# A convolution, Gram and batch-norm kernel: filter weights loaded with z, two idle products, and the first channel's second convolution in two halves

## The chip, the cores and the metric

The kernel runs on one core of a Trainium2 chip. The core has TensorE (matrix products; PE in the profile, with its weight loads shown apart as PEld), VectorE (DVE), ScalarE (ACT), GpSimd (POOL) and SyncE (SP), and 16 DMA engines that move data between device memory and the on-chip memory. The metric is the device time of one execution in microseconds (us). The runs of the kernel before took 885.52, 881.20 and 883.17 us, so the median is 883.17 us.

## The reference, cut to what matters

The input x has 4 images, 64 channels and 256 x 256 pixels. Layer 0 convolves every channel with a filter that is a product of a vector over rows and a vector over columns. Both vectors come from a small network with sine activations that is applied to 256 positions:

```python
def filt(z, w1, b1, w2, b2, w3, b3, wo, freq, t, deltas):     # z: 256 x 33
    h = sin(freq * (z @ w1 + b1))
    h = sin(freq * (h @ w2 + b2))
    h = sin(freq * (h @ w3 + b3))
    return (h @ wo) * exp(-t * abs(deltas))                    # 256 x 64 channels
hx, hy = filt(z, X...), filt(z, Y...)
k = outer(hx[:, c], hy[:, c])                                  # per channel
y = causal_conv2d(x, k) / 512 + x * bias[c]                    # by FFT in the reference
# layer 1
scores = y @ y.T / sqrt(256)                                   # per image and channel
y2 = y + (scores * weights[c]).sum(-1, keepdims=True)
out = batch_norm(y2) * gamma[c] + beta[c]                      # mean and variance per channel
```

## The kernel before

Since the filter is an outer product, a convolution is two products with triangular Toeplitz matrices, one along each axis. They are built of 64 x 64 blocks; the product of a block of rows with a block that would be zero is left out. All numbers are 32-bit floats, and one product in the code is two weight loads and two matmuls in the profile.

**Start.** Loads go out on two queues: SP's (`nc.sync`) and ScalarE's (`nc.scalar`). SP issues z^T (L85), the biases (L89), two decay tables (L99, L101), the image data `xt` of channel 0 in four parts (L72), a unit matrix, per-channel constants, the weights `w` of channel 0 and the image data of channel 1. ScalarE issues the first layer's weights (L87) and then the weights of the other layers (L90). Both networks, X and Y, run side by side as one block-diagonal network of 128 rows, in two halves of 128 positions. In each of three layers TensorE makes a product `ph` (L131), DVE adds the bias, scales to turns and takes off whole turns in three steps (L134 to L139; the scale `turns` is made from the biases at L123), and ScalarE takes the sine (L141). Then TensorE makes the filter rows of channel 0, repeated on all partitions (L147, a = 1 for the first convolution and then a = 0 for the second), and DVE multiplies each by its decay (L150). Four transfers (L155), two on each queue, lay the shifted copies out as channel 0's Toeplitz matrix `toep` on 64 partitions, and DVE copies it to the other 64 (L163). The filters of all channels (L158, L161) are written to device memory (L170), from where the other channels' matrices are read. Three products whose results nobody reads (`idle`, L167) stand on TensorE between this and the first convolution.

**Per channel.** `conv_z` makes the first convolution (L210) in two halves m of the result, and `copy_z` has ScalarE copy each half from PSUM (the matmul results' memory) to `z`, one copy for each half u of the partitions (L219). `conv_x0` makes the second convolution from z (L233): for each half m of the result and each block i it sums over four blocks k of z; k = 0, 1 are the first half of z and k = 2, 3 the second. DVE then adds bias times x (L240). `gram` makes the Gram blocks (L270), DVE weighs and sums them (L290 to L304), GpSimd sums over partitions (L312), and two channels later mean and variance are formed, and ScalarE normalizes and stores (L366, L406).

**Order.** The schedule is written out by hand: each engine works its instructions in the order of the code. In the loop of channel c, ScalarE first copies channel c + 1's Toeplitz matrix to the upper partitions (`copy_h`, L192); then come `conv_x0(c)`, `conv_z(c + 1)` and `gram(c)` on TensorE. The four loads of a Toeplitz matrix (`load_h`, L187) go on SP's queue, each between other loads; those of channel 1 stand before the loop. The eight PSUM banks after the start belong to one pool, `ps`, that hands them out in turn.

Of the kernel before, what the change touches and what calls it, by code (L numbers as in the profile page):

```python
# [8 lines left out]
F32 = mybir.dt.float32  # L9
AF = mybir.ActivationFunctionType  # L10
ALU = mybir.AluOpType
# [4 lines left out]
B, C, S = 4, 64, 256  # L16
P = 128
EMB = 33
# [3 lines left out]
H = P // 2  # L22
# [15 lines left out]
def conv_scores_bn_kernel(  # L38
# [1 line left out]
    tc: tile.TileContext,  # L40
    xT: bass.AP,
    wl: bass.AP,
    zT: bass.AP,
    fw: bass.AP,
    fb: bass.AP,
    decay: bass.AP,
# [11 lines left out]
    nc = tc.nc  # L58

    const = ctx.enter_context(tc.tile_pool(name="const", bufs=1))  # L60
# [5 lines left out]
    xts, ws, hs = {}, {}, {}  # L66
# [14 lines left out]


    ctx.enter_context(tc.manual_schedule())
    zT_sb = const.tile([EMB, S], F32, name="zT_sb")
    nc.sync.dma_start(zT_sb, zT)  # L85
    fw_sb = const.tile([P, 4, P], F32, name="fw_sb")
    nc.scalar.dma_start(fw_sb[:EMB, 0, :], fw[:EMB, 0, :])  # L87
    fb_sb = const.tile([P, 4], F32, name="fb_sb")
    nc.sync.dma_start(fb_sb, fb)  # L89
    nc.scalar.dma_start(fw_sb[:, 1:, :], fw[:, 1:, :])  # L90
    eps = const.tile([P, 1], F32, name="eps")
    nc.vector.memset(eps, BN_EPS)
    ones = const.tile([P, H], F32, name="ones")
# [12 lines left out]
    chan_sb = const.tile([P, 3, C], F32, name="chan_sb")  # L106
# [15 lines left out]
    with tc.tile_pool(name="fps", bufs=4, space=PSUM) as fps:  # L122
        nc.vector.tensor_scalar(turns, fb_sb[:, 3:4], 1.0 / (2.0 * math.pi), None, ALU.mult)  # L123

        halves = [zT_sb[:, bass.ts(n, P)] for n in range(2)]
        for layer in range(3):
            for n in range(2):
                rhs = halves[n]
                K = rhs.shape[0]
                ph = fps.tile([P, P], F32, tag="ph", name=f"ph_{layer}_{n}")  # L130
                nc.tensor.matmul(ph, lhsT=fw_sb[:K, layer, :], rhs=rhs, start=True, stop=True)  # L131

                a = wk.tile([P, P], F32, tag="fa", name=f"fa_{layer}_{n}")
                nc.vector.tensor_scalar(  # L134
                    a, ph, fb_sb[:, layer : layer + 1], turns, ALU.add, ALU.mult
                )
                k = wk.tile([P, P], F32, tag="fk", name=f"fk_{layer}_{n}")
                nc.vector.tensor_scalar(k, a, ROUND, None, ALU.add)  # L138
                nc.vector.scalar_tensor_tensor(a, k, ROUND, a, ALU.subtract, ALU.subtract)  # L139
                h = wk.tile([P, P], F32, tag="fh", name=f"fh_{layer}_{n}", bufs=4)  # L140
                nc.scalar.activation(h, a, AF.Sin, scale=-PI2)  # L141
                halves[n] = h
        for a in (1, 0):
            ph = fps.tile([P, S], F32, tag="ph0", name=f"ph0_{a}", bufs=3)
            for n in range(2):
                weights = fw_sb[:, 3, a * C : a * C + 1].to_broadcast([P, P])
                nc.tensor.matmul(  # L147
                    ph[:, bass.ts(n, P)], lhsT=weights, rhs=halves[n], start=True, stop=True
                )
            nc.vector.tensor_tensor(g0_sb[:, a, :S], ph, decay0_sb[:, a], ALU.mult)  # L150
            for n in range(2):
                row = g0_sb[H * n : H * n + 1, a, 32 * n :]
                src = bass.AP(row.tensor, row.offset, [row.ap[0], [1, 32], [1, S]])
                queue = nc.scalar if n else nc.sync
                queue.dma_start(hs[0][bass.ts(n, 32), a, :S], src)  # L155
        ph = fps.tile([P, S], F32, tag="ph0", name="ph_out", bufs=3)
        for n in range(2):
            nc.tensor.matmul(  # L158
                ph[:, bass.ts(n, P)], lhsT=fw_sb[:, 3, :], rhs=halves[n], start=True, stop=True
            )  # L160
        nc.vector.tensor_tensor(g_sb[:, :S], ph, decay_sb, ALU.mult)  # L161
        for a in (1, 0):
            nc.vector.tensor_copy(hs[0][H:, a, :S], hs[0][:H, a, :S])  # L163

        for n in range(3):
            idle = fps.tile([P, 3, P], F32, tag="idle", name=f"idle_{n}", bufs=1)
            nc.tensor.matmul(idle, lhsT=fw_sb[:, 3, :], rhs=fw_sb[:, 1:, :], start=True, stop=True)  # L167
    for a in (1, 0):
        queue = nc.scalar if a else nc.sync
        queue.dma_start(  # L170
# [25 lines left out]
    ps = ctx.enter_context(tc.tile_pool(name="ps", bufs=8, space=PSUM))  # L196

    st8, zs = {}, {}
# [22 lines left out]
    def conv_x0(c, z, parts=range(2)):  # L221


        xt = [xts[c, v] for v in range(2)]
        toep, x0 = hs[c], st8[c][0]
        for m in parts:
            p2 = [ps.tile([P, 2, S], F32, tag="ps", name=f"p2_{c}_{m}_{v}") for v in range(2)]
            for i in range(2):
                for k in range(4):
                    for t in range(4):  # L230
                        v, u = t % 2, t // 2
                        rows = bass.ts(v, H)
                        nc.tensor.matmul(  # L233
                            p2[v][bass.ts(u, H), i, : S - H * k],
                            lhsT=z[rows, u, k, bass.ts(2 * m + i, H)],
                            rhs=toep[rows, 0, H * k : S], start=(k == 0), stop=(k == 3),
                        )
            for v in range(2):
                part = bass.ts(m, 2)
                nc.vector.scalar_tensor_tensor(  # L240
                    x0[:, v, part], xt[v][:, part], chan_sb[:, 0, c : c + 1],
                    p2[v][:, :, ::-1], ALU.mult, ALU.add,
                )

    def begin(c):
        x0 = wk.tile([P, 2, 4, S], F32, tag="x0", name=f"x0_{c}", bufs=5)
# [192 lines left out]
    def last_channels(c):  # L439
# [6 lines left out]
        copy_h(c)  # L446
        finish(*fins[e - 1], 0, 1)
        conv_x0(p, zs.pop(p))
        load_w(c)
        minus_mean(moms[f])  # L450
# [25 lines left out]
        tot = sum_squares(q, mom_q)  # L476
        z = zs.pop(c)
        conv_x0(c, z, [0])
        mom_p = sm.tile([P, 8], F32, tag="mom", name=f"mom_{p}")
        add_red_of(p, 0, red_by_pe(p, 0), mom_p)  # L480
        conv_x0(c, z, [1])
        finish(*fins[e], 1, 0)
        finish(*fins[e], 1, 1)
# [62 lines left out]
    for c in range(C - 2):  # L546
        p, q, f, e = c - 1, c - 2, c - 3, c - 4
# [115 lines left out]
```

## Time and profile before

| | |
|---|---|
| runs | 885.52, 881.20, 883.17 us; median 883.17 us |
| profiled execution | 879.23 us, of which the span from first to last instruction is 877.3 us |
| granted TensorE clock, mean | 0.992 |
| TensorE busy / weight loads / DVE / ACT / POOL | 98% / 95% / 86% / 71% / 48% of the span |
| first matmul of the filter network | 2.69 us after the span's start |
| first product of channel 0's convolution | 15.96 us |
| first product of channel 1's convolution after the wait | 25.73 us |

The profile shows one execution. Its busy shares say how much of the span an engine worked. Its chain follows back from the last instruction what released each step. A row of the timeline has the start, the duration, the engine (a q behind the name is the engine's instruction queue, which issues transfers), the line, the operation, the tiles written and read, and in brackets how long the engine had been idle and what ended that. A row of the waits says who waited for whom, for how long in total, how often, and the longest. Tiles are named without their numbers, so `g0_sb` appears as `g_sb` and `decay0_sb` as `decay_sb`.

### The profile page before, as it was taken

To read this page: it belongs to the slowest core of one execution; us is meant where nothing else is said; L and a number is where in the kernel's file an instruction comes from. 1 tells how busy PE (TensorE), PEld (TensorE's weight loads), DVE (VectorE), ACT (ScalarE), POOL (GpSimd) and SP (SyncE) were. 2 spreads that over 40 slices of the span, in tenths; PEclk is the share of its full clock that TensorE was granted. 3 is DMA by queue.
4 is the path that set the end of the run, shared out by engine and by line. 5 is a ranking of instruction groups with operands and counts; after the bars stand their busy time and mean duration, and the time that the engine had idled before them with its cause. 6 is when DMAs were issued, how large, how long until landed. Compare 5 with 4: busy or idle time off the path is not lost.

```text
span 877.3 us, 55962 instructions
## 1 busy us (share of the span) xinstructions
PE 857.4 (98%) x24678; PEld 836.7 (95%) x24678; DVE 754.9 (86%) x2642; ACT 620.6 (71%) x1212; POOL 425.1 (48%) x195
## 2 busy tenths in 40 slices
PE   7999999999999999999999999999999999999993
PEld 5999999999999999999999999999999999999992
DVE  3578988988988898898898898898898898898885
ACT  2256767867777777777777777776776777776784
POOL 0236446446546546545545545645645645645600
PEclk9999999999999999999999999999999999999996
DMA  6623556565565655555555556555555555556534
GB/s 187 214 84 133 199 197 207 198 208 196 200 205 196 205 203 199 199 202 204 195 200 203 200 202 206 198 202 201 197 205 197 198 200 205 204 192 213 177 138 169
DMA packets 89914, 169.69 MB, mean 193 GB/s; under 512 B 10566, under 2 KB 11784, under 8 KB 89672
## 3 DMA queue, kind: packets, MB, share of 16 engines
q1 hardware_dynamic: 89116, 165.51, 54.8%
q8 instruction: 194, 3.18, 1.5%
q10 hardware_dynamic: 556, 0.61, 0.2%
q14 instruction: 48, 0.39, 0.1%
HBM read 98.18 MB, written 67.76 MB: 189 GB/s over the span
## 4 chain that ended last, share of the span: by engine, by line
PE 97%; DVE 1%; DMA 1%; ACT 0%; issue 0%; ACTq 0%; DVEq 0%
PE p L210 32%; PE g L270 32%; PE p L233 32%; PE rp L341 1%; PE rp L346 0%; DMA toep<-g_sb 0%; PE ph L131 0%; DVE x L355 0%; ACT o L406 0%; DMA fw_sb<-in_fw 0%; DVE fa L134 0%; DVE fa L139 0%; ACT z L219 0%; ACT fh L141 0%; DVE fk L138 0%
## 5 line engine op out<-in xcount | busy, mean ns | idle before, releaser
L312 POOL PARTITION_ALL_REDUCE rd<-sp x61 | 373.5, 6122 | 183.5 <-DVE sp L304 183.5
L233 PE MATMUL p<-toep,z 64*64 64x256 f32 (+3 forms) x8192 | 301.8, 296 | 0.1
L210 PE MATMUL p<-toep,xt 64*64 64x256 f32 (+3 forms) x8192 | 301.7, 296 | 0.1
L270 PE MATMUL g<-x 64*64 64x192 f32 (+1 forms) x8192 | 300.4, 296 | 0.1
L233 PEld LDWEIGHTS p<-toep,z 64*64 64x64 f32 x8192 | 292.5, 133 | 7.2 <-ACT z L219 0.6
L210 PEld LDWEIGHTS p<-toep,xt 64*64 64x64 f32 x8192 | 289.4, 133 | 7.4 <-PE idle L167 0.7
L270 PEld LDWEIGHTS g<-x 64*64 64x64 f32 x8192 | 287.6, 133 | 0.7 <-issue 0.4
L290 DVE SCALAR_TENSOR_TENSOR junk<-g,w 128x192 f32<-128x192 f32 x512 | 161.2, 352 | 82.7 <-PE g L270 82.7
L406 ACT ACTIVATE o<-x,sh,g 128x512 f32<-128x512 f32 x253 | 204.2, 811 | 3.1
L240 DVE SCALAR_TENSOR_TENSOR x<-xt,chan_sb,p 128x512 f32<-128x512 f32 x256 | 174.0, 741 | 8.1 <-PE p L233 8.1
L219 ACT COPY z<-p 128x512 f32<-128x512 f32 x256 | 134.4, 575 | 24.7 <-PE p L210 24.7
L366 ACT ACTIVATE sq<-x,mom 128x1024 f32<-128x1024 f32 x128 | 146.3, 1143 | 5.3 <-DVE x L355 2.0
L326 DVE SCALAR_TENSOR_TENSOR x<-x,rd 128x1024 f32<-128x1024 f32 x122 | 144.2, 1220 | 0.1
L304 DVE SCALAR_TENSOR_TENSOR sp<-eye_sb,red,pr 128x128 f32<-128x128 f32 x488 | 138.0, 345 | 0.0
L330 POOL PARTITION_ALL_REDUCE mom<-mom x61 | 24.3, 399 | 230.5 <-DVE x L326 226.4
L319 ACT COPY rd<-rd 64x512 f32<-64x512 f32 x61 | 37.5, 615 | 135.9 <-POOL rd L312 135.9
L294 DVE SCALAR_TENSOR_TENSOR pr<-g,w 128x256 f32<-128x256 f32 x256 | 107.6, 420 | 0.0
L192 ACT COPY toep<-toep 64x512 f32<-64x512 f32 x63 | 38.9, 617 | 33.1 <-DMA toep<-g_dram 24.2
L361 ACT ACTIVATE mom<-mom 128x1 f32<-128x1 f32 x62 | 18.2, 293 | 35.3 <-POOL mom L330 35.0
L290 DVE DVE_READ_ACCUMULATOR junk<-g,w 128x1 f32 x512 | 42.7, 83 | 0.0
L372 POOL PARTITION_ALL_REDUCE tot<-mom x62 | 29.7, 480 | 9.4 <-ACT sq L366 9.4
L366 ACT ACTIVATION_READ_ACCUMULATOR sq<-x,mom 128x1 f32 x128 | 23.9, 187 | 0.0
(60 smaller groups left out, 210.2 us busy)
## 6 DMA issues: line engine op xcount, KB each, us to landing
xt<-in_xT SPq DMA_DIRECT2D x256, 256.0 KB
out<-o SPq DMA_DIRECT2D x256, 256.0 KB
w<-in_wl SPq DMA_DIRECT2D x64, 320.0 KB
toep<-g_dram SPq DMA_DIRECT2D x252, 36.0 KB
g_dram<-g_sb SPq DMA_DIRECT2D x1, 320.0 KB
g_dram<-g_sb ACTq DMA_DIRECT2D x1, 320.0 KB
decay_sb<-in_decay SPq DMA_DIRECT2D x1, 256.0 KB
fw_sb<-in_fw ACTq DMA_DIRECT2D x1, 192.0 KB
```

The costliest lines, as they stand in the source:

```text
L210: nc.tensor.matmul(p1[u][bass.ts(v, H), k, : S - H * i], lhsT=xts[c, v][rows, i, bass.ts(2 * m + k, H)], rhs=toep[rows, 1, H * i : S], sta ...
L219: nc.scalar.copy(zs[c][:, u, bass.ts(m, 2), :], p1[u][:, :, ::-1])
L233: nc.tensor.matmul(p2[v][bass.ts(u, H), i, : S - H * k], lhsT=z[rows, u, k, bass.ts(2 * m + i, H)], rhs=toep[rows, 0, H * k : S], start=(k ...
L240: nc.vector.scalar_tensor_tensor(x0[:, v, part], xt[v][:, part], chan_sb[:, 0, c : c + 1], p2[v][:, :, ::-1], ALU.mult, ALU.add,)
L270: nc.tensor.matmul(gs[u][bass.ts(h, H), o, :], lhsT=xb[rows, v, i, m, :], rhs=xb[rows, v, i, t, :], start=(i == 0), stop=(i == 3),)
L290: nc.vector.scalar_tensor_tensor(junk, g[:, part, :], 1.0 / math.sqrt(S), w[:, 3 * n : 3 * n + 3, :], ALU.mult, ALU.mult, accum_out=red0[: ...
L294: nc.vector.scalar_tensor_tensor(pr[:, b].rearrange("p (t s) -> p t s", s=H), g[:, COL, :], 1.0 / math.sqrt(S), w[:, 6:10, :], ALU.mult, A ...
L304: nc.vector.scalar_tensor_tensor(sp[:, b, part], eye_sb, red0[:, b, n : n + 1], pr[:, b, part], ALU.mult, ALU.add,)
L312: nc.gpsimd.partition_all_reduce(rd.rearrange("p b s -> p (b s)"), sp.rearrange("p b s -> p (b s)"), P, RED.add)
L326: nc.vector.scalar_tensor_tensor(x0[:, v], x0[:, v], 1.0, rd[:, 2 * v, None, :].to_broadcast([P, 4, S]), ALU.mult, ALU.add, accum_out=mom[ ...
L366: nc.scalar.activation(sq, st8[c][0][:, v], AF.Square, bias=mom[:, 5:6], accum_out=mom[:, 6 + v : 7 + v])
L406: nc.scalar.activation(o, y, AF.Identity, bias=sh, scale=g)
```

## The change

Three things are changed. First, the host packs the first layer's weights and z^T into one array `zw`, which one transfer on SP's queue brings; the biases go first on ScalarE's queue, followed by the other three weights as one array. Second, two idle products are made instead of three. Third, `conv_x0` of channel 0 is a function of its own: it opens the PSUM tiles of both halves m at once, makes all products with the first half of z (k = 0, 1), and then all with the second (k = 2, 3), with the bias added to each m as soon as it is complete. The other channels keep their order; their bias addition moves to `add_bias`.

```diff
 
 
     ctx.enter_context(tc.manual_schedule())
-    zT_sb = const.tile([EMB, S], F32, name="zT_sb")
-    nc.sync.dma_start(zT_sb, zT)
-    fw_sb = const.tile([P, 4, P], F32, name="fw_sb")
-    nc.scalar.dma_start(fw_sb[:EMB, 0, :], fw[:EMB, 0, :])
+    zw_sb = const.tile([P, P + S], F32, name="zw_sb")
+    nc.sync.dma_start(zw_sb[:EMB], zw[:EMB])
     fb_sb = const.tile([P, 4], F32, name="fb_sb")
-    nc.sync.dma_start(fb_sb, fb)
-    nc.scalar.dma_start(fw_sb[:, 1:, :], fw[:, 1:, :])
+    nc.scalar.dma_start(fb_sb, fb)
+    fw_sb = const.tile([P, 3, P], F32, name="fw_sb")
+    nc.scalar.dma_start(fw_sb, fw)
     eps = const.tile([P, 1], F32, name="eps")
     nc.vector.memset(eps, BN_EPS)
     ones = const.tile([P, H], F32, name="ones")
...
     with tc.tile_pool(name="fps", bufs=4, space=PSUM) as fps:
         nc.vector.tensor_scalar(turns, fb_sb[:, 3:4], 1.0 / (2.0 * math.pi), None, ALU.mult)
 
-        halves = [zT_sb[:, bass.ts(n, P)] for n in range(2)]
+        halves = [zw_sb[:EMB, bass.ts(1 + n, P)] for n in range(2)]
         for layer in range(3):
             for n in range(2):
                 rhs = halves[n]
-                K = rhs.shape[0]
+                weights = fw_sb[:, layer - 1, :] if layer else zw_sb[:EMB, :P]
                 ph = fps.tile([P, P], F32, tag="ph", name=f"ph_{layer}_{n}")
-                nc.tensor.matmul(ph, lhsT=fw_sb[:K, layer, :], rhs=rhs, start=True, stop=True)
+                nc.tensor.matmul(ph, lhsT=weights, rhs=rhs, start=True, stop=True)
 
                 a = wk.tile([P, P], F32, tag="fa", name=f"fa_{layer}_{n}")
                 nc.vector.tensor_scalar(
...
         for a in (1, 0):
             ph = fps.tile([P, S], F32, tag="ph0", name=f"ph0_{a}", bufs=3)
             for n in range(2):
-                weights = fw_sb[:, 3, a * C : a * C + 1].to_broadcast([P, P])
+                weights = fw_sb[:, 2, a * C : a * C + 1].to_broadcast([P, P])
                 nc.tensor.matmul(
                     ph[:, bass.ts(n, P)], lhsT=weights, rhs=halves[n], start=True, stop=True
                 )
...
         ph = fps.tile([P, S], F32, tag="ph0", name="ph_out", bufs=3)
         for n in range(2):
             nc.tensor.matmul(
-                ph[:, bass.ts(n, P)], lhsT=fw_sb[:, 3, :], rhs=halves[n], start=True, stop=True
+                ph[:, bass.ts(n, P)], lhsT=fw_sb[:, 2, :], rhs=halves[n], start=True, stop=True
             )
         nc.vector.tensor_tensor(g_sb[:, :S], ph, decay_sb, ALU.mult)
         for a in (1, 0):
             nc.vector.tensor_copy(hs[0][H:, a, :S], hs[0][:H, a, :S])
 
-        for n in range(3):
+        for n in range(2):
             idle = fps.tile([P, 3, P], F32, tag="idle", name=f"idle_{n}", bufs=1)
-            nc.tensor.matmul(idle, lhsT=fw_sb[:, 3, :], rhs=fw_sb[:, 1:, :], start=True, stop=True)
+            nc.tensor.matmul(idle, lhsT=fw_sb[:, 2, :], rhs=fw_sb, start=True, stop=True)
     for a in (1, 0):
         queue = nc.scalar if a else nc.sync
         queue.dma_start(
...
     def conv_x0(c, z, parts=range(2)):
 
-        xt = [xts[c, v] for v in range(2)]
-        toep, x0 = hs[c], st8[c][0]
+        toep = hs[c]
+        if not c:
+            first_x0(z)
+            return
         for m in parts:
             p2 = [ps.tile([P, 2, S], F32, tag="ps", name=f"p2_{c}_{m}_{v}") for v in range(2)]
             for i in range(2):
...
                             lhsT=z[rows, u, k, bass.ts(2 * m + i, H)],
                             rhs=toep[rows, 0, H * k : S], start=(k == 0), stop=(k == 3),
                         )
-            for v in range(2):
-                part = bass.ts(m, 2)
-                nc.vector.scalar_tensor_tensor(
-                    x0[:, v, part], xt[v][:, part], chan_sb[:, 0, c : c + 1],
-                    p2[v][:, :, ::-1], ALU.mult, ALU.add,
-                )
+            add_bias(c, m, p2)
+
+    def add_bias(c, m, p2):
+        for v in range(2):
+            part = bass.ts(m, 2)
+            nc.vector.scalar_tensor_tensor(
+                st8[c][0][:, v, part], xts[c, v][:, part], chan_sb[:, 0, c : c + 1],
+                p2[v][:, :, ::-1], ALU.mult, ALU.add,
+            )
+
+    def first_x0(z):
+
+        toep = hs[0]
+        p2 = [
+            [ps.tile([P, 2, S], F32, tag="ps", name=f"p2_0_{m}_{v}") for v in range(2)]
+            for m in range(2)
+        ]
+        for half in range(2):
+            for m in range(2):
+                for i in range(2):
+                    for k in range(2 * half, 2 * half + 2):
+                        for t in range(4):
+                            v, u = t % 2, t // 2
+                            rows = bass.ts(v, H)
+                            nc.tensor.matmul(
+                                p2[m][v][bass.ts(u, H), i, : S - H * k],
+                                lhsT=z[rows, u, k, bass.ts(2 * m + i, H)],
+                                rhs=toep[rows, 0, H * k : S],
+                                start=(i == 0 and k == 0), stop=(i == 1 and k == 3),
+                            )
+                if half:
+                    add_bias(0, m, p2[m])
 
     def begin(c):
         x0 = wk.tile([P, 2, 4, S], F32, tag="x0", name=f"x0_{c}", bufs=5)
...
     dec = np.exp(-(deltas[:, None] * t[None])).astype(np.float32)
     decay = np.concatenate([dec, dec / np.float32(FFT)], 0)
 
-    fw = np.zeros((P, 4, P), np.float32)
+    zw = np.zeros((P, P + S), np.float32)
+    zw[:EMB, P:] = a["L0_conv_z"][0, ::-1].T
+    fw = np.zeros((P, 3, P), np.float32)
     fb = np.zeros((P, 4), np.float32)
     for i, n in enumerate("XY"):
         lo, hi = i * C, (i + 1) * C
-        fw[:EMB, 0, lo:hi] = a[f"L0_conv_{n}w1"]
-        fw[lo:hi, 1, lo:hi] = a[f"L0_conv_{n}w2"]
-        fw[lo:hi, 2, lo:hi] = a[f"L0_conv_{n}w3"]
-        fw[lo:hi, 3, lo:hi] = a[f"L0_conv_{n}wo"]
+        zw[:EMB, lo:hi] = a[f"L0_conv_{n}w1"]
+        fw[lo:hi, 0, lo:hi] = a[f"L0_conv_{n}w2"]
+        fw[lo:hi, 1, lo:hi] = a[f"L0_conv_{n}w3"]
+        fw[lo:hi, 2, lo:hi] = a[f"L0_conv_{n}wo"]
         for j, b in enumerate(("b1", "b2", "b3")):
             fb[lo:hi, j] = a[f"L0_conv_{n}{b}"]
         fb[lo:hi, 3] = a[f"L0_conv_{n}freq"][0]
...
     arrays = {
         "xT": xo.transpose(2, 1, 0, 5, 4, 3).reshape(C, 2, P, 4, S),
         "wl": wl,
-        "zT": a["L0_conv_z"][0, ::-1].T,
+        "zw": zw,
         "fw": fw,
         "fb": fb,
         "decay": decay[:, ::-1],
```

More of the change, by code (lines that the diff above doesn't have):

```diff
@@ L42, in conv_scores_bn_kernel @@
     wl: bass.AP,
-    zT: bass.AP,
+    zw: bass.AP,
     fw: bass.AP,
```

## The prediction

> **What bounds the kernel now.** I read the page's busy shares and its chain first, then the waits of TensorE, then the first 26 us as a timeline, because every line of the change acts there.
>
> ```profile
> PE 857.4 (98%) x24678; PEld 836.7 (95%) x24678; DVE 754.9 (86%) x2642; ACT 620.6 (71%) x1212; POOL 425.1 (48%) x195
> ...
> PE 97%; DVE 1%; DMA 1%; ACT 0%; issue 0%; ACTq 0%; DVEq 0%
> ```
>
> TensorE is busy for 98% of the span and carries 97% of the chain. From 52 us on its pieces repeat every 13.08 us (52.42, 65.50, 78.58 in the chain). So the end moves by what TensorE loses or wins before it settles into that rhythm, and by nothing else. The waits that ended TensorE's idle times, over the whole run, with totals in us, times and the longest:
>
> ```profile
> PE ph L131 <- DMA fw_sb<-in_fw: 2.7, 1, 2.7
> ...
> PEld p L233 <- ACT z L219: 0.6, 2, 0.3
> ...
> PEld p L210 <- ACT toep L192: 0.3, 1, 0.3
> ```
>
> The first is the load of the filter network, the second the x0 product of channel 0 waiting for z, the third the z product of channel 1 waiting for its Toeplitz matrix. After 26 us no wait of TensorE on a transfer is listed; the 2.4 us on DVE at L341 belong to the last channels, which stay as they are. The head of the timeline (start, duration, and in brackets the idle time before and what ended it):
>
> ```profile
> 0.72 0.64 ACTq L87 DMA_DIRECT2D fw_sb<-in_fw  x1
> 0.72 0.43 SPq L85 DMA_DIRECT2D zT_sb<-in_zT  x1
> ...
> 1.22 0.37 SPq L89 DMA_DIRECT2D fb_sb<-in_fb  x1
> ...
> 2.69 1.22 PE L131 MATMUL ph<-zT_sb,fw_sb 33*128 33x128 f32 x4 [2.69 <-DMA fw_sb<-in_fw]
> ...
> 3.66 0.15 DVE L123 TENSOR_SCALAR turns<-fb_sb 128x1 f32<-128x1 f32 x1 [2.50 <-DMA fb_sb<-in_fb]
> 3.93 0.41 DVE L134 TENSOR_SCALAR fa<-ph,fb_sb,turns 128x128 f32<-128x128 f32 x1
> ```
>
> The chain names TensorE ahead of the first fa at 3.93, but a product is two of the four matmuls, and cut at 3.2 us the timeline has the first two done after 0.79 us, at 3.48. What really came last is the bias load: it landed just before 3.66, turns took 0.15, and fa followed. Next, the pieces of the chain before 26 us that lie around the first Toeplitz matrix:
>
> ```profile
> 12.04 3.56 DMA toep<-g_sb
> 15.60 0.02 issue
> 15.62 0.30 DVE toep L163
> 15.92 0.04 issue
> 15.96 4.67 PE p L210 x128
> 20.62 1.06 ACT z L219 x2
> ```
>
> The transfer takes 3.56 us from its issue; the idle products (13.04, 2.86 us, so until 15.90) end just as the DVE copy does (15.91). Then the timeline around the step to channel 1:
>
> ```profile
> 25.06 0.62 ACT L192 COPY toep<-toep 64x512 f32<-64x512 f32 x1 [3.38 <-DMA toep<-g_dram]
> ...
> 25.73 0.40 PEld L210 LDWEIGHTS p<-toep,xt 64*64 64x64 f32 x10 [0.31 <-ACT toep L192]
> ```
>
> TensorE could have gone on at 25.42 and was held to 25.73 by a Toeplitz matrix whose last load landed shortly before 25.06.
>
> **Part 1, the loads.** SP loses the issues of zT (0.43) and the biases (0.37) and gains one of zw (0.43); ScalarE's queue still issues two, now the biases and the three other weights. The first matmul waited for the load issued on ScalarE's queue with 0.64 us of issue; the one on SP cost 0.43, so I put zw's landing, with rows half as long again, 0.15 us before 2.65. Products done: 2.69 - 0.15 + 0.79 = 3.33. The biases are issued at 0.72 instead of 1.22; at the same 2.44 us to landing they arrive at 3.16, turns and its gap to fa (3.93 - 3.66 = 0.27) end at 3.43. So fa starts at 3.43: 0.5 us sooner. Both ends: 0, if the biases or zw land as late as before, or if the big weight load, now beside a decay load that SP issues 0.41 us sooner, holds the second layer (first use 5.32 before, 4.8 then; no wait on it shows today); 0.7 if the biases take the 1.93 us of the load that was first on that queue and zw gains the whole 0.21. A loss up to 0.2 stays possible where the single load on few rows is slow. I take 0.5, as two rows point to it. ScalarE's own first work at 4.96 (then 4.4) lies behind its table load and warm-up, which end at 3.28: no price.
>
> The Trainium skill, "DMA: Bandwidth & Descriptors", section "Issuing engines are not separate DMA queues", says that issuing on another engine saves only the issuing sequencer's time. By it the biases gain the 0.5 us of queueing and no more, where the row of the first load on that queue would give 1.0; fa is then bound by the products within 0.1 us of it.
>
> **Part 2, two idle products.** The layers, DVE and ScalarE steps from 3.93 to 12.04 are a strict chain and keep their lengths, so toep is issued at 11.53. SP is free by then: its last wait, for w, ended before 11.0. The DMA engines are 56% and 38% busy from 12 to 14 us, no full backlog, so the 3.56 us stay and the first z product starts at 15.46. Ends: 0 (landing kept at 15.60 by the channel 1 loads) and 0.5. Three idle products would end at 15.40; two end about 14.4, or 14.9 if the first one is slower. Removing 0.97 us of them wins nothing here, as the transfer covers it; it opens a pause of 0.6 to 1.0 us on TensorE. Whether that costs clock:
>
> ```profile
> L167 PEld LDWEIGHTS idle<-fw_sb x6: 186/189/333, 12.8 to 15.1; 128*128 128x128 f32 x6
> ...
> L158 PEld LDWEIGHTS ph_out<-fh,fw_sb x4: 333/333/333, 12.0 to 12.6; 128*128 128x128 f32 x4
> ```
>
> Weight loads take 333 ns up to 12.83 and 186 to 189 from 14.02: the clock rises between them, after some 3 us of closely packed matmuls. I price the shorter filler at 0, ends 0 and +4.7 (the whole first product, 4.67 us, at half speed); 0 is nearer, as the packed matmuls from 9.84 are all still there.
>
> The Trainium skill, "TensorE: Matmul & The Clock Gate", Part 1, speaks against this edit: the clock is released only after a busy window of about 3.4 us that runs free of the kernel. By its rule the pause alone is harmless, but a window that catches the pause could put the release off; an estimate from the page is up to 1.7 us lost (half of 3.4), where the trace gives 0.
>
> **Part 3, x0 of channel 0.** Today products for k = 2, 3 stand in the first quarter of x0, and TensorE waits 0.28 and 0.29 us for the two copies of the second half of z. In the new order all products of k = 0, 1 go first: (256 + 192)/640 of the columns, 0.70 of about 4.36 us, so 3.05 us of work, while the copies end 1.31 us after x0 begins (21.68 against 20.37). The 0.57 us go. The bias additions on DVE (two of 0.75 us per half, first at 23.40) come in one group near 23.6 and end about 26.6; the Gram products need them at 28.8 or later, and DVE is otherwise idle. The four banks of PSUM open together leave the other four to z of channel 1, freed by copies long done: 0.
>
> **Part 4, what is late next.** TensorE reaches z of channel 1 at 25.42 - 0.5 - 0.57 = 24.35. Its Toeplitz copy, the end of a chain that starts at the filter's last product, moves by 0.5: it ends at 25.18 and TensorE goes on at 25.23. Then 0.57 of Part 3 turns into a longer wait and the gain is 0.50. But the last of its four loads, issued by 21.83 (four issues of 2.68 us from 19.15), landed some 3 us later, and in 22.5 to 24.5 us this lay among the packets:
>
> ```profile
> q8 instruction: 1, 0.02, 3.8%
> ```
>
> One instruction fetch, 3.8% of 16 engines over 2 us: 1.2 us on one engine; narrower cuts put its start at 23.0. The page's 3.18 MB of such packets are 64 bytes for each of TensorE's 2 x 24678 instructions, so I take them as its program, fetched as it proceeds. At 23.0 TensorE stood half way through x0; in the new order half of the instructions are done 3.05 us after x0's start at 19.87, at 22.9, almost as before, while the loads are 0.5 sooner. If they pass ahead of it, the copy is ready by about 24.3 and the gain is 25.73 - 24.35 = 1.38.
>
> **Sum.** Loads 0.50; idle products 0; x0 up to 0.57; the wait at 25.42 gives back between -0.57 and +0.31. Total 0.50 to 1.38, and I take 0.9, between the two. The profiled execution took 879.23 us (span 877.3 and 1.9 around it), so 878.3; it lies 3.9 us under the median of the runs, 883.17, and I subtract the same 0.9 from that: 882.3.
>
> **Rivals.** (a) The gain stops at the loads: the Toeplitz matrix of channel 1 arrives only 0.5 sooner, -0.5, 882.7. For it: the 3.38 us that ScalarE waited for it. Against: the fetch that lay in its way. (b) The change does nothing: landings of biases or of toep are set by the traffic beside them (DMA 0.92 to 1.04 busy from 3 to 6 us), 0 to -0.2, 883.1. (c) Slower: the clock is not yet granted when the pause comes, and the first z product runs at half speed. Each cold us costs 0.5, so it decides from 1.8 us on; the full 4.67 us would give +4.7 - 0.9 = 3.8, 887.0. For it: the clock rose only about 13 us. Against: it rose before the last two idle products.
>
> **Numbers.** A change under 0.5%, 4.4 us, is about what a measurement of this kernel can't tell from none; all the startup edits together are worth a third of that. Forecast (-0.6 to -1.4) 0.42, (a) 0.32, (b) 0.13, (c) 0.07, and 0.06 for a larger gain that only repeated slow starts could bring, such as cold idle products before that delayed the first product. The three runs of before spread over 4.3 us and the profiled one lies 2 below them, which is wider than the cases: 879.2 to 885.0. The chances: same 0.89, faster 0.07 (the last case and spread), slower 0.04 (half of (c), where the slow stretch outlasts the first product).
>
> **What would show it.** First fa near 3.4; first z product near 15.5, TensorE idle 0.6 to 1.0 us before it; no wait on z in x0 of channel 0; the wait on the Toeplitz copy before z of channel 1 either gone or near 0.9; from there the same 13.08 us rhythm. Wrong would be: fa still at 3.9, weight loads of 333 ns scaled into the first z product, or a rhythm other than 13.08.

## The result and the profile after

The changed kernel takes 881.90 us (median of 22 runs, 878.34 to 887.44) against 882.93 us for the kernel before (22 runs, 879.94 to 895.25). The ratio is 0.9992 with a 95% interval of 0.9978 to 1.0007: no difference that these runs can tell from none. The profiled execution took 878.34 us with a span of 876.5 us, against 879.23 and 877.3.

The head of the timeline of the changed kernel (start, duration, engine, line, operation, in brackets the idle time before and what ended it):

```profile
0.72 0.41 ACTq L87 DMA_DIRECT2D fb_sb<-in_fb  x1
...
1.15 0.45 ACTq L89 DMA_DIRECT2D fw_sb<-in_fw  x1
...
2.54 1.22 PE L130 MATMUL ph<-zw_sb 33*128 33x128 f32 x4 [2.54 <-DMA zw_sb<-in_zw]
2.69 0.15 DVE L122 TENSOR_SCALAR turns<-fb_sb 128x1 f32<-128x1 f32 x1 [1.53 <-DMA fb_sb<-in_fb]
...
3.37 0.41 DVE L133 TENSOR_SCALAR fa<-ph,fb_sb,turns 128x128 f32<-128x128 f32 x1 [0.52 <-PE ph L130]
...
4.93 1.53 PE L130 MATMUL ph<-fh,fw_sb 128*128 128x128 f32 x4 [1.18 <-DMA fw_sb<-in_fw]
...
11.62 1.37 SPq L154 DMA_DIRECT2D toep<-g_sb  x2
...
12.62 3.06 PE L166 MATMUL idle<-fw_sb 128*128 128x384 f32 x4
...
15.47 0.29 DVE L162 COPY toep<-toep 64x256 f32<-64x256 f32 x1 [2.18 <-DMA toep<-g_sb]
...
15.74 4.60 PE L209 MATMUL p<-toep,xt 64*64 64x256 f32 x125
...
20.23 4.48 PE L263 MATMUL p<-toep,z 64*64 64x256 f32 x124
...
24.03 0.62 ACT L191 COPY toep<-toep 64x512 f32<-64x512 f32 x1 [2.51 <-DMA toep<-g_dram]
...
24.70 4.52 PE L209 MATMUL p<-toep,xt 64*64 64x256 f32 x122
...
29.00 0.33 PE L297 MATMUL g<-x 64*64 64x192 f32 x1
```

Three things are to be seen. The first fa (DVE's first step behind the network's first product) is at 3.37 instead of 3.93 and now waits for the product, not for the biases. A new wait stands behind it: the second layer's matmul at 4.93 is released by the weights, which the kernel before never waited for. And two idle products take 3.06 us here where three took 2.86 before, because the clock rose only at 15.42 instead of 13.25; so they end at 15.68 and leave no pause at all. The x0 product runs without a wait for z, and the first Gram product of channel 0 comes at 29.00 instead of 29.88.

That is 0.88 us at the head, and the spans differ by 0.78. The agreement is chance. Between the Gram product of channel 0 and the z product of channel 3 the changed kernel gains another 0.37 (22.17 us before, 21.80 after); over the next 57 channels it loses 1.42 (745.85 us, 747.27); from the first Gram product of the last channel to the end it gains 0.95 (25.96, 25.01). Those last three pieces differ as much between executions of one kernel: the loss in the middle is 0.3, 9.6 and 2.3 us in three of the kernel before (table below), and the last stretch took 25.96 us in x0_only and 25.02 in loads_only. The loss shows in TensorE's waits, and one stretch of 13 us holds most of it; first the waits of the changed kernel from 26 to 860 us:

```profile
PEld p L209 <- issue: 1.1, 2, 0.9
PEld p L234 <- issue: 0.4, 2, 0.3
...
```

Then two stretches of the changed kernel, and the last one of each kernel (busy time of PE, PEld, DVE, ACT, POOL, then granted clock, DMA share and GB/s):

```profile
600.00:612.00 12.00, 12.00 (x360) 11.77 (x351) 10.64 (x36) 9.54 (x20) 6.52 (x2) 1.00 0.58 197
612.00:625.00 13.00, 12.47 (x358) 11.80 (x353) 10.60 (x40) 9.37 (x20) 6.92 (x3) 1.00 0.63 203
860.00:876.50 16.50, 2.35 (x22) 1.32 (x18) 9.46 (x37) 8.37 (x16) 1.60 (x4) 0.77 0.41 159
```

```profile
860.00:877.30 17.30, 3.25 (x22) 1.81 (x18) 9.46 (x37) 8.20 (x16) 1.59 (x4) 0.59 0.39 152
```

From 612 to 625 us TensorE issues 358 matmuls; the kernel before has 390 in the same stretch. "Issue" says that the engine waited for nothing that the profile shows. These are the two long waits, from the timeline of TensorE's weight loads:

```profile
612.25 1.51 PEld L234 LDWEIGHTS p<-toep,z 64*64 64x64 f32 x47 [0.27 <-issue]
...
617.37 1.61 PEld L209 LDWEIGHTS p<-toep,xt 64*64 64x64 f32 x48 [0.88 <-issue]
```

In the last stretch both do 22 matmuls, in 2.35 us at a mean clock of 0.77 and in 3.25 us at 0.59: the clock's fall came before the last products in one execution and after them in the other.

### The profile page after: what moved, and what is told of

It is laid out like the page before. It is cut to its first block, busy times and chain, and to the rows that moved or that the text cites. A ratio compares the mean times of both kernels' runs of the same rounds, so it can differ in the third digit from the quotient of the medians.

```text
span 876.5 us, 55956 instructions
## 1 busy us (share of the span) xinstructions
PE 856.5 (98%) x24676; PEld 841.9 (96%) x24676; DVE 754.8 (86%) x2642; ACT 620.5 (71%) x1212; POOL 425.4 (49%) x195
## 4 chain that ended last, share of the span: by engine, by line
PE 97%; DVE 1%; DMA 0%; ACT 0%; issue 0%; ACTq 0%; DVEq 0%
PE g L297 32%; PE p L209 32%; PE p L234 31%; PE p L263 0%; DMA fw_sb<-in_fw 0%; PE rp L368 0%; PE rp L373 0%; PE idle L166 0%; DVE x L382 0%; ACT o L433 0%; PE ph L146 0%; PE ph L130 0%; DVE fa L133 0%; DVE junk L317 0%; DVE fa L138 0%
## 5 line engine op out<-in xcount | busy, mean ns | idle before, releaser
L209 PE MATMUL p<-toep,xt 64*64 64x128 f32 (+3 forms) x8192 | 303.7, 297 | 0.6 <-issue 0.5
L234 PE MATMUL p<-toep,z 64*64 64x128 f32 (+3 forms) x8064 | 298.9, 296 | 0.0
```

Of the source, the lines that this page charges most:

```text
L209: nc.tensor.matmul(p1[u][bass.ts(v, H), k, : S - H * i], lhsT=xts[c, v][rows, i, bass.ts(2 * m + k, H)], rhs=toep[rows, 1, H * i : S], sta ...
L234: nc.tensor.matmul(p2[v][bass.ts(u, H), i, : S - H * k], lhsT=z[rows, u, k, bass.ts(2 * m + i, H)], rhs=toep[rows, 0, H * k : S], start=(k ...
```

## The experiments

A difference of 1 us can't be timed among runs that spread over 9, so the runs were read by their profiles. The table holds all of them, one profiled execution each; before_again and before_third are the kernel before once more, after_again and after_third the changed kernel, and the others are described below. The columns are the starts of fa and of the first Toeplitz transfer, the moment at which the trace's clock record has the clock rise, the end of the idle products, the first z product, the time from there to the first Gram product, and TensorE's loss between channels 3 and 60 against 57 times 13.08 us. All in us.

| run | fa | transfer | clock rises | idle end | first z | z to Gram | loss |
|---|---|---|---|---|---|---|---|
| before | 3.93 | 12.03 | 13.25 | 15.90 | 15.96 | 13.92 | 0.3 |
| before_again | 3.63 | 11.74 | 13.29 | 15.78 | 15.83 | 13.59 | 9.6 |
| before_third | 3.96 | 12.06 | 15.72 | 17.03 | 17.08 | 13.60 | 2.3 |
| loads_only | 3.38 | 11.80 | 15.19 | 16.63 | 16.69 | 14.03 | 1.4 |
| idles_only | 3.52 | 11.63 | 12.92 | 14.56 | 15.36 | 14.23 | 0.8 |
| x0_only | 3.48 | 11.60 | 15.08 | 16.47 | 16.53 | 13.15 | 1.1 |
| bias_queue | 4.35 | 12.46 | 14.92 | 16.90 | 16.95 | 13.68 | 4.7 |
| after_three | 3.40 | 12.15 | 13.75 | 16.20 | 16.26 | 13.73 | 3.9 |
| after | 3.37 | 11.62 | 15.42 | 15.69 | 15.74 | 13.26 | 1.7 |
| after_again | 3.44 | 11.66 | 14.80 | 15.40 | 15.45 | 13.73 | 0.9 |
| after_third | 3.39 | 12.04 | 15.22 | 15.80 | 15.86 | 13.76 | 1.0 |
| after_none | 3.39 | 11.78 | 18.92 | none | 15.51 | 15.16 | 5.4 |
| fw_second | 3.37 | 11.47 | 15.56 | 15.68 | 15.73 | 13.28 | 0.2 |
| few_stores | 3.36 | 11.68 | 16.04 | 15.88 | 15.94 | 13.18 | 1.7 |

The theory at the outset was the prediction's: loads 0.5, idle products 0, x0 the rest, with an instruction fetch in the way of the last Toeplitz load. The rivals were that the transfers behind the loads hide them, that channel 1's Toeplitz matrix takes back what x0 wins, and that the shorter filler costs clock.

### The loads alone

```diff
 # the changed kernel, with three idle products and the old conv_x0
-        for n in range(2):
+        for n in range(3):
```

> Only the packed load and the queue of the biases are changed; three idle products and the old order of x0 stay. Measured by the starts of the first fa (3.93 us before, 3.37 in the changed kernel), the first z product of channel 0 (15.96, 15.74) and the first Gram product of channel 0 (29.88, 29.00). My theory: the loads are worth 0.4 to 0.5 us at fa and at the issue of the first Toeplitz transfer (12.03 before, so 11.6), 0.2 to 0.4 of it at the first z product unless the third idle product ends after the Toeplitz copy; TensorE still waits 0.5 to 0.6 us for z in x0; first Gram product at 29.4 to 29.7. Rival, that the loads change nothing behind the transfer: first z product 15.9 to 16.0 and Gram product 29.9.

fa came at 3.38, 0.05 sooner than the expected range, and the transfer at 11.80, 0.2 later than expected. The first z product at 16.69 met neither expectation: the idle products ended after the copy. The Gram product came at 30.72, a microsecond past the range and later than in the kernel before.

```profile
5.11 1.38 PE L130 MATMUL ph<-fh,fw_sb 128*128 128x128 f32 x4 [1.34 <-DMA fw_sb<-in_fw]
...
12.81 3.82 PE L166 MATMUL idle<-fw_sb 128*128 128x384 f32 x6
...
15.36 0.29 DVE L162 COPY toep<-toep 64x256 f32<-64x256 f32 x1 [1.88 <-DMA toep<-g_sb]
```

These lines of its timeline carry both readings: the weights release the second layer at 5.11, where the sine was ready 0.3 us before, and three idle products take 3.82 us and end at 16.63, a microsecond after the copy.

### Two idle products alone

```diff
-        for n in range(3):
+        for n in range(2):
             idle = fps.tile([P, 3, P], F32, tag="idle", name=f"idle_{n}", bufs=1)
```

> Only the third idle product is left out. My theory: nothing, where the clock rises near 13 us as in the profile before: first z product at 15.96, first Gram product at 29.9, TensorE idle about 1 us before the z product. Where the clock rises later (15.42 us in the profile of the changed kernel), the two products take 1.5 us each and end at 16.1, 0.2 after the copy. Rival, the pause delays the clock into the z product: weight loads of the first z products above the 133 ns of before, and a Gram product at 30.5 or later.

The clock rose at 12.92, the two products ended at 14.56, and the first z product came at 15.36, after a pause of 0.8 us; no clock was lost. But it came 0.6 sooner than expected: the transfer was issued at 11.63 and not at 12.03, which is 0.4, and the product started on the transfer's landing while the DVE copy still ran (15.21 to 15.50), where in the kernel before the third idle product had lasted until the copy's end. The Gram product, at 29.59, came 0.3 sooner than expected. With the loads of the kernel before untouched, the bias scale started at 2.86 here:

```profile
2.86 0.15 DVE L123 TENSOR_SCALAR turns<-fb_sb 128x1 f32<-128x1 f32 x1 [1.70 <-DMA fb_sb<-in_fb]
3.52 0.41 DVE L134 TENSOR_SCALAR fa<-ph,fb_sb,turns 128x128 f32<-128x128 f32 x1 [0.51 <-PE ph L131]
```

The first prediction's 3.66 was one draw.

### x0 alone

```diff
 # the kernel before, with the changed kernel's conv_x0, add_bias and first_x0
+        if not c:
+            first_x0(z)
+            return
```

> Only x0 of channel 0 is made in the new order; loads and three idle products stay. My theory: TensorE no longer waits for z in x0 (0.57 us before); the instruction fetch that began at 23.0 us comes 0.4 or more later against the four Toeplitz loads of channel 1, which now pass ahead of it, so ScalarE's copy of that matrix starts at 24.0 to 24.5 instead of 25.06, and the first Gram product at 29.1 to 29.3 instead of 29.88. Rival (a), the Toeplitz matrix of channel 1 holds TensorE: copy at 25.06 as before, a wait of about 0.9 us on it, Gram product at 29.8 to 29.9.

No wait for z, no wait for the Toeplitz matrix: ScalarE's copy began at 23.57, 0.4 sooner than the expected range, and from the first z product to the first Gram product it took 13.15 us, the shortest of all. The Gram product itself, at 29.68, missed the expected 29.1 to 29.3, as three idle products held the first z product to 16.53. The early copy does not show that the order moved the fetch out of the way: in before_again, with the old order, it began at 23.64.

### The changed kernel again

> The changed kernel once more, to see what in one profile of it is its own and what belongs to the execution. My theory: fa at 3.37, no wait for z in x0, first Gram product 28.9 to 29.1 again; the moment at which the clock rises (15.42 us), the 1.2 us that TensorE lost between 600 and 625 us and the moment at which the clock falls at the end (868.8 us) differ from execution to execution by up to 1 to 2 us each. Rival: they come at the same places, and belong to the change.

fa 3.44, no wait for z, Gram product at 29.18, 0.1 outside the expected range: ScalarE's copy began at 24.36, and TensorE waited 0.38 us for it.

```profile
24.36 0.62 ACT L191 COPY toep<-toep 64x512 f32<-64x512 f32 x1 [3.02 <-DMA toep<-g_dram]
...
25.03 0.21 PEld L209 LDWEIGHTS p<-toep,xt 64*64 64x64 f32 x8 [0.38 <-ACT toep L191]
```

So rival (a) is right in some executions. The clock rose 0.6 us sooner than in the first profile. The lost time in the middle, 0.9 against 1.7, lay at the same two channels, 45 and 46: on that count the rival did better than my expectation.

### The kernel before again

> The kernel before once more. In two kernels that keep its loads, the bias scale started at 2.86 and 3.12 us and the first Toeplitz transfer was issued at 11.6; in the one profile of before it was 3.66 and 12.03. My new theory: that late landing of the biases (3.6 us) belonged to one execution, so here the bias scale starts near 2.9 to 3.2, fa near 3.5, and the transfer is issued at 11.6 to 11.7, as in the changed kernel (11.62, 11.66). Rival, the first prediction's reading: 3.6, 3.9 and 12.0 again. Where the clock rises after 14.5 us, the third idle product ends at 16.4 to 16.6 and holds the first z product; first Gram product then at 30.4 to 30.8, else 29.5.

The bias scale started at 3.37, fa at 3.63, the transfer was issued at 11.74: between the two theories, and no repeat of 3.66 and 12.03. The third execution below did repeat them. The clock rose at 13.29 and the Gram product came at 29.42, as expected for that. This and the next three ran on another chip, where the kernel before took 887.49 us; its loss in the middle was 9.6 us. The losses go with the chip: the four profiles taken there lost 3.9 to 9.6 us, the other ten 0.2 to 2.3.

### Three idle products in the changed kernel

> The changed kernel with three idle products. My theory: what the third product costs depends on when the clock rises: near 13 us nothing (first z product at 15.4 to 15.5, first Gram product 29.0); from 14.5 us on about 1 us (16.5 to 16.7, Gram product 29.9 to 30.2). Rival: nothing in either case.

The clock rose at 13.75, between the two cases. The products ended at 16.20 and the copy at 16.01: 0.2 us lost. With loads_only, x0_only, bias_queue and the two repeats of before this makes a row: from the transfer's issue to the first z product, three idle products give 3.93, 4.09, 4.11, 4.49, 4.93, 4.89 and 5.02 us as the clock rises at 13.25, 13.29, 13.75, 14.92, 15.08, 15.19 and 15.72; two give 3.73 to 4.26 from 12.92 to 16.04.

### No idle product

```diff
-        for n in range(2):
+        for n in range(0):
```

> The changed kernel without any idle product. My theory: the closely packed matmuls then last only from 9.4 to 12.8 us, the clock rises in most executions only after the z product has started, its first weight loads take 270 ns instead of 133, and the first Gram product is 0.5 to 2 us later than 29.0. Rival, idle products do nothing for the clock: first Gram product 28.8 to 29.2.

As expected, but for the first weight loads, which took 225 ns and not 270: the clock rose only at 18.92, in the first z product, which took 6.25 us instead of 4.60; the Gram product came at 30.67. Its timeline:

```profile
15.54 6.25 PE L209 MATMUL p<-toep,xt 64*64 64x256 f32 x122 [2.54 <-DMA toep<-g_sb]
```

So the filler is worth having: from the transfer's issue to the Gram product this execution took 18.89 us, and five with two idle products 17.38 to 17.58.

### The biases' queue alone

```diff
-    nc.scalar.dma_start(fw_sb[:EMB, 0, :], fw[:EMB, 0, :])
     fb_sb = const.tile([P, 4], F32, name="fb_sb")
-    nc.sync.dma_start(fb_sb, fb)
+    nc.scalar.dma_start(fb_sb, fb)
+    nc.scalar.dma_start(fw_sb[:EMB, 0, :], fw[:EMB, 0, :])
     nc.scalar.dma_start(fw_sb[:, 1:, :], fw[:, 1:, :])
```

> The kernel before with the biases first on ScalarE's queue, ahead of both weight loads; z and the first layer's weights stay two loads, three idle products, old order of x0. My theory: the biases land at 2.7, but the first layer's weights, now second on that queue, at 2.9 to 3.1, so fa is at 3.7 to 3.9: no better than the 3.48 to 3.52 of undisturbed loads in the old order. Rival, the biases alone set fa: 3.4.

The direction was right and the size too small: fa came at 4.35. The biases were there at 2.6, but the first layer's weights, one place further back, released the first matmul only at 3.55:

```profile
3.55 1.19 PE L131 MATMUL ph<-zT_sb,fw_sb 33*128 33x128 f32 x4 [3.55 <-DMA fw_sb<-in_fw]
```

The two edits of the loads belong together: moving the biases ahead pays only if nothing urgent is pushed back.

### The other weights ahead of the decay tables

```diff
     fw_sb = const.tile([P, 3, P], F32, name="fw_sb")
-    nc.scalar.dma_start(fw_sb, fw)
+    nc.sync.dma_start(fw_sb, fw)
```

> The changed kernel with the array of the three other weights issued on SP, directly behind the packed load and ahead of the decay tables, instead of second on ScalarE's queue. In the changed order these weights landed at 4.8 to 5.3 us (4.06 to 4.46 before) and held the second layer. My theory: ahead of the decay tables on the same queue they land at 3.6 to 4.3, the second layer starts as soon as its sine is done (4.76), and the first Toeplitz transfer is issued at 11.4 to 11.5 instead of 11.62 to 12.15. Rival, the order on the queues does not matter for them: landing at 4.8 or later, transfer at 11.6 or later.

As expected: the second layer started with its sine, and the transfer was issued at 11.47, sooner than in any other run.

```profile
4.76 1.70 PE L130 MATMUL ph<-fh,fw_sb 128*128 128x128 f32 x4 [1.01 <-ACT fh L140]
...
11.47 1.37 SPq L154 DMA_DIRECT2D toep<-g_sb  x2
```

From fa to the transfer this run needs 8.10 us, as the loads of the kernel before do (8.10 to 8.12 in five runs); the changed loads need 8.22 to 8.75. The first z product gained nothing from it, since with the clock rising at 15.56 two idle products ended at 15.68. This is one execution.

### Fewer stores, and both kernels beside it

```diff
-        nc.sync.dma_start(out[c, v, n], o)
+        if c % 8 == 0 or c >= C - 4:
+            nc.sync.dma_start(out[c, v, n], o)
```

> The changed kernel without the stores of most channels: only every eighth channel and the last four are written, so the output is incomplete and about 59 of 168 MB are not moved. Everything before the stores is computed. My theory: the 0.3 to 9.6 us that TensorE loses between channel 3 and channel 60 against a rhythm of 13.08 us come from instruction fetches that the data transfers delay; with a third of the traffic gone the loss is below 0.3 us. Rival, they come from TensorE itself or from elsewhere on the chip: the loss is that of the changed kernel next to it.

> The changed kernel on the same chip as the two above. My theory: transfer issued at 11.6 to 12.2, first Gram product 29.0 to 29.5, a loss of 0.3 us or more between channels 3 and 60.

> The kernel before on the same chip. My theory: transfer issued at 11.6 to 12.1, so no later than in the changed kernel; first Gram product 29.4 to 29.9 where the clock rises near 13 us, 30.4 to 30.8 where it rises after 14.5; a loss of 0.3 us or more between channels 3 and 60.

My theory that a third less traffic would end the loss fell: without those stores (54.5 MB, not the 59 expected) TensorE lost 1.7 us, the changed kernel beside it 1.0, the kernel before 2.3. In all three most of TensorE's waits of that stretch are put down to issue. The packets of the instruction queue bear out the other half of the theory, the fetches: in the 14 profiles, from 32 to 838 us, all 59 waits of TensorE's weight loads that lasted 0.2 us or more and are put down to issue end 1.2 to 1.6 us behind the end of an instruction fetch, although a fetch comes only every 4.3 us and a moment taken at random would lie there in 11% of cases. In the changed kernel the fetches from 609.90 to 610.86 and from 613.80 to 615.98 us stand before the waits that end at 612.25 and 617.37; what makes such a fetch late stays open. The heads went as expected, but for the Gram product of the changed kernel, 0.1 later than the range: biases on SP late again (scale at 3.69, transfer at 12.06), the changed loads no better at the transfer (12.04), the Gram product at 29.62, and 30.68 for the kernel before, whose clock rose at 15.72.

## Why the prediction was right or wrong

The time, 882.3 for 881.9, and the call of no difference were right. The time alone proves little: the interval of the ratio allows changes from -1.9 to +0.6 us, which takes in the forecast and rivals (a) and (b). By the profiles the head gained about what the sum said: first Gram product at 29.88, 29.42 and 30.68 in three profiles of the kernel before, mean 29.99; at 29.00, 29.18 and 29.62 after, mean 29.27; 0.73 where 0.9 was forecast, from three executions each that spread over 1.26 and 0.62 us. But two of the terms were wrong, and it is luck that they cancelled.

**Part 1, the loads: 0.5 forecast, 0.0 measured.** The step that failed is taking the biases' 2.44 us to landing as a property of the load. In five executions of the old loads the scale started at 2.86, 3.12, 3.37, 3.66 and 3.69, so fa came at 3.70 on average; in eight of the new it started within 2.69 to 2.76, fa at 3.39. That gain of 0.3 is real. The prediction then named the other end, the weights of the second layer held up by a decay load issued sooner, and gave it no weight: the wait for these weights cost 0.1 to 0.65 us in every execution, and among the changed loads it is gone only in fw_second, where they go ahead of the decay tables on one queue. At the issue of the Toeplitz transfer the old loads stand at 11.81 on average (five runs) and the new ones at 11.82 (seven).

**Part 2, the idle products: 0 forecast, about 0.5 measured.** The step that failed is "removing 0.97 us of them wins nothing here". It holds only where the clock rises near 13 us, as in the one profile at hand: from the transfer to the Gram product the kernel before took 17.85 us there and idles_only 17.96. Where it rises after 14.9 us, an idle product takes 1.55 us until it does, the third one ends up to 1.1 us after the Toeplitz copy, and TensorE's first real work waits for a product that nobody reads. From transfer to first z product it is 4.49 us on average with three (seven runs) and 4.00 with two (six). This difference depends on how often the clock rises late: it did in four of the seven and in five of the six, and among those alone it is 4.83 against 4.05. The pause that Part 2 feared appeared in none of the profiles of the changed kernel, which all had a late clock; in idles_only, where the clock was early, it came and cost nothing. Rival (c) did not come up: it needs the pause and a late clock together, and in the five profiles with two idle products and a late clock, the products lasted until behind the transfer's landing. after_none shows what a cold first product costs.

The Trainium skill, "TensorE: Matmul & The Clock Gate", Part 1, has the clock released by a window of about 3.4 us that runs free of the kernel. The moments seen with a filler, 12.92 to 16.04 us, spread over 3.1 us and agree with that. The clock's own record shows the step: in all 14 profiles the stretch at full clock lasts 846.51, 849.92, 853.33, 856.75 or 860.16 us, each 3.41 more than the last. The prediction used the rule only for what it might cost in the changed kernel, and not for the kernel before, where it cost more.

**Parts 3 and 4, x0 and the wait behind it: 0.4 forecast, 0.4 measured.** The 0.57 us wait for z is gone wherever the new order ran. It was worth 0.44 and not 0.57: from x0's first product to the next z product the old order takes 4.81 to 4.83 us in five of six runs, the new 4.37 in five of eight. From the first z product to the first Gram product the old order takes 13.84 us on average (six runs), the new 13.44 (seven, without after_none). The new order has two groups, 13.15 to 13.28 and 13.73 to 13.76; in the second channel 1's Toeplitz matrix holds TensorE for 0.38 us, as rival (a) has it. The instruction fetch as its cause is not shown: in after_again the last load took 3.4 us with a fetch of 1.6 us beside it, but in after_three it took 3.75, and the next fetch began only 0.1 us before it had landed.

**Rival (b)** described Part 1 rightly in its effect: one late load was exchanged for another. Its cause, the traffic beside the loads, is neither shown nor refuted, since the weights that came late were issued within 0.1 us of a decay table (1.15 and 1.22 us in the changed kernel).

## What to carry to other kernels

A duration from one profile is one draw: before a wait on a small transfer or on a clock change is booked as a gain, ask how it came out in other executions, and put its spread in the range. When a load is moved forward, the one that is pushed back is the first place to look, and when the engine that matters runs filler, the filler's price is set by the slowest state it may run in. A span that moves by the expected amount proves little; cut it into stretches and see that each moved for the reason given. And a wait that is put down to issue is worth laying beside the packets of the instruction queue.

## What the runs showed of the hardware

A load of 2 KB, second on its queue, started the work behind it anywhere from 2.86 to 3.69 us in five executions; first on the other queue from 2.69 to 2.76 in eight (and at 2.62 in bias_queue). The Trainium skill, "DMA: Bandwidth & Descriptors", section "Issuing engines are not separate DMA queues", gives another queue no more than the time of issue; here the issue came 0.5 us sooner and the use 0.1 to 1.0.

TensorE lost 0.2 to 9.6 us in the middle of otherwise equal executions, mostly in pieces of 0.2 to 1.0 us for which the profile names no releaser but issue, and which end 1.2 to 1.6 us behind a fetch of TensorE's own instructions. Where it is large, this is more than the change is worth; one execution without a third of the transfers lost 1.7 us, inside the range of the others on its chip (0.2 to 2.3).

From the last channel's first Gram product to the end it takes 25.89 to 25.97 us in the five executions in which the clock fell before the last products or as they began, 25.00 to 25.08 in the eight in which it fell after them, and 25.69 in one in between. As the stretch at full clock has lengths in steps of 3.41 us, up to 0.95 us of an execution depend on where such a step ends.
